# Attention on one core: paired projections, key copies and means on ScalarE, sums set per block

## The chip, the cores and the metric

The kernel runs on one core of a Trainium2 chip. The metric is the device time of one execution in microseconds (us), less is better. Four engines matter here: TensorE (PE) multiplies matrices from SBUF into PSUM, VectorE (DVE) does elementwise arithmetic, ScalarE (ACT) does functions such as exp and copies, and SyncE (SP) issues transfers. Each engine runs its own queue of instructions in order and waits on semaphores for the others.

## The reference

The input x has the shape (16, 384, 16, 16) in fp32. Four layers follow each other.

```
L0  attention over 2 groups of 8 frames: N = 2048 tokens, 12 heads of 32
    qk = xt @ qk_w.T;  v = xt                      (values are the input itself)
    attn = softmax(q k^T / sqrt(32))
    attn = alpha * I + beta * attn - gamma / N     (per head)
    out  = attn @ v
L1  y = depthwise 7x7(x);  layer norm over channels
    y = gelu(y @ w1 + b1)                          (384 -> 1536)
    y = grn(y)       norms of each channel over the pixels, relative to their mean
    x = x + y @ w2 + b2                            (1536 -> 384)
L2  Sobel x and y, 1x1 fusion (768 -> 384), layer norm, gelu, x = x + ...
L3  bn, 1x1, depthwise 3x3, bn, 1x1, residual; linear attention with
    phi(t) = exp(0.5 (2t - t^2)), 8 heads of 48, residual; layer norm, MLP, residual
```

## The kernel before

The input is held as 8 blocks (b, i) of 512 columns, 4 for each of the 2 groups, each as three tiles of 128 channels. Everything is fp32. A matmul of fp32 shows as two instructions in the profile. All engine work is issued through the helper `InOrder` (line 97), which pins each engine's program order to the order of emission, so almost all rows of the profile carry L97 and are told apart by their tiles.

**Attention** (`attention`, lines 395 to 586). There are 6 units (2 groups by 3 sets of 128 channels, 4 heads each). A unit has 4 blocks of 512 queries (numbered 0 to 23 over all units), and a block has 16 key steps. In a key step `scores` makes the scores of 4 heads (tiles st, two banks each, from a pool of 3), and ScalarE turns the two tiles into exponentials e. Then `weighted` works on the step before: 4 matmuls into av, and two VectorE adds that sum the exponentials of several steps into s. `ADDS` (line 56) says how many steps are summed into one group: 4 everywhere before. A group's sum goes through matmuls with ones into dn, the softmax denominators: four quarters of 128 columns in four later steps, or the whole 512 columns in step 2 of the next block for a block's last group (lines 496 to 506). A dictionary `due` holds what is to be emitted at a later step. At the end of a block ScalarE copies av (va) and scales x (xg), step 2 of the next block copies dn (r), and VectorE inverts and scales in the steps behind it; ScalarE passes over r once more (junk) with an accumulated sum as a check of the range.

Queries and keys of the next unit are projected meanwhile: `SLOTS` (line 32) names the key steps of each of a unit's blocks behind which one projection stands (3 fp32 matmuls into the first bank of a tile of the same pool of 3, then a copy: queries on ScalarE, keys on VectorE). The values are transferred as they are. `channel_means` (lines 225 to 238) sums the channels for the gamma term on VectorE, for both groups.

The function `fill` (lines 1466 to 1496) slips other work into the attention's steps where a model of VectorE's time (`pace`) leaves room: first the 7x7 convolution of the blocks (0, 0) and (0, 1) in single VectorE and ScalarE instructions, and, once block (0, 0) is done, its normalization (task l1_0_0; sums su and sv on TensorE).

**The rest** is a list of tasks for every block: l1 (layer 1), mid (layers 2 and 3 up to the linear attention), l3c (the last MLP), and the remaining convolutions. `Plan.all` (line 181) orders them before the kernel is built: of the operations that can start within `SLACK` of the earliest, it takes that of the task with the smallest `RANK`. The MLP weights are loaded in turns: `TURNS` (line 35) lists which layer's weights are in and for which blocks, and `AFTER` delays the convolution's later tiles until a named operation is done. Names used below: ph and po are the first and second MLP matmul, gs is the sum over gelu outputs and pg its matmul, pc and pd are the 1x1 convolutions of layer 3, s0_l, su_l and sv_l belong to a layer norm.

A second branch of the program, a general attention for inputs out of range, is not executed.

Of the kernel before, what the change touches and what calls it, by code (L numbers as in the profile page):

```python
# [15 lines left out]
P = 128  # L16
# [12 lines left out]
NBLK = N // BLK  # L29
NIP = NBLK  # L30
NQC = N // P
SLOTS = ((0, 4, 8), (0, 4), (0, 4), (0,))
FIRST = NQC + 10

TURNS = (
    (0, ((0, 0), (0, 1), (0, 2),)),
    (1, ((0, 0),)),
    (0, ((0, 3),)),
    (1, ((0, 2),)),
    (0, ((1, 0),)),  # L40
    (1, ((0, 1),)),
    (0, ((1, 1), (1, 2), (1, 3),)),
    (1, ((0, 3), (1, 0), (1, 3), (1, 2), (1, 1),)),
)
AFTER = ('hid', 0, 2, 1)

RANK = {
    "mid": ((-2.0, 20.2, -65.9, 40.3), (11.6, 63.7, 50.6, 36.1)),
    "l1": ((-41.0, 15.6, 6.7, 64.2), (55.1, 56.5, 16.9, 27.6)),
    "l3c": ((32.8, 24.4, 106.0, 83.3), (3.4, 80.2, 74.5, 60.5)),  # L50
    "conv": 100.5,
}
SLACK = 0.151
JUNK = 2

ADDS = (4,) * 24
XB, YB, SB = 12, 2, 22
TB = BLK // P
RB = 2 * HW
# [27 lines left out]
class InOrder:  # L87


    def __init__(self, tc, engine):  # L90
        self.tc, self.engine, self.last = tc, engine, None
# [103 lines left out]
def pace(t):  # L195


    n, i = divmod(t - 1, NQC)
    adds = ADDS[n]
    stride = adds // 4  # L200
    pe, dve = 2.066, 2.275 if t and i % adds else 0.0
    at = i - adds - 1
    if at >= 0 and at % adds % stride == 0 and at % adds < 4 * stride and i > adds:
        pe += 0.22
    elif i == 1 and n > 0:
        pe += 0.87
    else:
        pe += 0.09
    if n > 0:
        dve += {2: 0.88, 3: 0.88, 4: 0.88, 5: 0.88, 6: 0.6, 7: 0.66}.get(i, 0.0)  # L210
    return pe, dve


class Task:


    def __init__(self, name, rank, ops):
        self.name, self.rank, self.ops, self.at = name, rank, ops, None
        self.head = next(ops, None)

    def advance(self):
        self.at, self.head = self.head, next(self.ops, None)


def channel_means(dve, pool, X, cols, b):


    parts = pool.tile([P, NC, NBLK], F32, tag="parts", name=f"parts_{b}")
    gm = pool.tile([P, NC], F32, tag="gm", name=f"gm_{b}")

    def part(n):
        dve.tensor_reduce(parts[:, :, n], X[b][n], AX.X, ALU.add)

    def whole():
        dve.tensor_reduce(gm, parts, AX.X, ALU.add)
        dve.scalar_tensor_tensor(gm, gm, -1.0 / N, cols("gamma"), ALU.mult, ALU.mult)

    return gm, [*(lambda n=n: part(n) for n in range(NBLK)), whole]


# [147 lines left out]
def attention(tc, X, xt, L0, block, small, col, cols, ones, load_qk, banks, fill, bound):  # L388
# [6 lines left out]
    with ExitStack() as actx:  # L395
# [15 lines left out]
        def projections(b, g):  # L411


            made = {w: [None] * NBLK for w in "qkv"}
            u = b * NC + g

            def qk(j, n):
                w = "qk"[j]
                pp = bank2(f"p{w}_{u}_{n}")
                for c in range(NC):  # L420
                    pe.matmul(
                        pp[:, 0, :],
                        wqk_sb[:, g, j, c, :],
                        X[b][n][:, c, :],
                        start=(c == 0),
                        stop=(c == NC - 1),
                    )
                o = made[w][n] = small(f"{w}_{u}_{n}")
                (act.copy if j == 0 else dve.tensor_copy)(o, pp[:, 0, :])
                return 2.7 - 0.6 * j  # L430

            def values(n):
                o = made["v"][n] = small(f"v_{u}_{n}")
                nc.sync.dma_start(o, xt[b, g, n])

            def key(n):
                values(n)
                return qk(1, n)

            step = lambda f, *a: lambda: f(*a)  # L440
            early = [step(key, 0), step(qk, 0, 0)] + [step(key, n) for n in range(1, NBLK)]
            late = [step(qk, 0, n) for n in range(1, NBLK)]
            return made, early, late

# [109 lines left out]

            return scores, weighted

        means = [channel_means(dve, op, X, cols, b) for b in range(NB)]
        for b, (_, steps) in enumerate(means):
            for i, s in enumerate(steps):
                due[b * NC * NBLK * NQC - 36 * b + 3 * i] = [s]  # L560
        made, early, late_steps = projections(*units[0])
        for s in early:
            s()
        before = None
        for u, (b, g) in enumerate(units):
            steps = late_steps
            scores, weighted = unit(u, made, means[b][0][:, g : g + 1])
            if u + 1 < len(units):
                made, early, late_steps = projections(*units[u + 1])
                steps = steps + early  # L570
            for n in range(NBLK):
                for t in range(NQC):
                    es = scores(n, t)
                    added = 0.0
                    if before:
                        before()
                    before = lambda f=weighted, a=(n, t, es): f(*a)
                    if t in SLOTS[n]:
                        added = steps.pop(0)() if steps else 0.0
                    fill((u * NBLK + n) * NQC + t, added)  # L580
            assert not steps
        before()
# [7 lines left out]
def conv_seq_kernel(  # L590
# [862 lines left out]
    for b in range(NB):  # L1453
        for i in range(NBLK):
            tasks.append(Task(f"mid_{b}_{i}", rank("mid", b, i), chain(layer2(b, i), layer3a(b, i), layer3b(b, i))))
            tasks.append(Task(f"l3c_{b}_{i}", rank("l3c", b, i), layer3c(b, i)))
            tasks.append(Task(f"l1_{b}_{i}", rank("l1", b, i), layer1(b, i)))
    lead = next(t for t in tasks if t.name == "l1_0_0")

    if fast:  # L1460
        open_pool("s", SB)
# [4 lines left out]
        def fill(t, added=0.0):  # L1466


            nonlocal lag
            if t < 0:  # L1470
                while plan.step(bias):
                    pass
                return
            if t % NQC == 9 and t > NQC:
                u, i = divmod(t // NQC - 1, NBLK)
                plan.mark(("l0", u // NC, i, u % NC))
            length, work = pace(t)
            free = length + added - work - lag
            if NC * NBLK * NQC - 36 < t <= NC * NBLK * NQC - 21 and t % 3 == 1:
                free -= 1.7  # L1480
            if ("y", 0, 0, NC - 1) in plan.made and t % 4 == 1 and plan.holds(lead, "wa"):
                if plan.step(lead) and lead.at.engine == "DVE":
                    free -= lead.at.length
            ops = []
            while t >= FIRST and ("y", 0, YB - 1, NC - 1) not in plan.made:
                op = conv.head
                if op.engine == "DVE":
                    if free < 0.4:
                        break
                    free -= op.length + 0.12 * (op.after[0] in ops[-1:])  # L1490
                if not plan.step(conv):
                    break
                ops.append(op)
                if op.engine == "ACT" and conv.head.engine == "DVE":
                    break
            lag = max(0.0, -free)

        attention(
# [133 lines left out]
```

## Time and profile before

| | |
|---|---|
| median of 3 runs | 2678.43 us (2677.66 to 2680.42) |
| profiled execution | 2678.47 us |
| its span | 2676.6 us |
| granted TensorE clock, mean | 0.997 |
| TensorE busy | 2644.7 us (99%) |
| VectorE busy | 1994.4 us (75%) |
| ScalarE busy | 1559.3 us (58%) |
| attention (first score matmul to last denominator) | 21.96 to 1044.70 us |

Busy times are shares of the span; matmuls are pipelined, so a busy TensorE is not a TensorE at its peak. A row of a group reads: line, engine, operation, output tile <- input tiles with their shapes, count | busy time, mean of one in ns | idle time of the engine just before, and what ended it. A row of the timeline reads: start, length in us, engine and operation, count, and in brackets an idle time before it with its releaser.

### The profile page before, as it was taken

To read this page: it belongs to the slowest core of one execution; us is meant where nothing else is said; L and a number is where in the kernel's file an instruction comes from. 1 tells how busy PE (TensorE), PEld (TensorE's weight loads), DVE (VectorE), ACT (ScalarE), POOL (GpSimd) and SP (SyncE) were. 2 spreads that over 40 slices of the span, in tenths; PEclk is the share of its full clock that TensorE was granted. 3 is DMA by queue.
4 is the path that set the end of the run, shared out by engine and by line. 5 is a ranking of instruction groups with operands and counts; after the bars stand their busy time and mean duration, and the time that the engine had idled before them with its cause. 6 is when DMAs were issued, how large, how long until landed. Compare 5 with 4: busy or idle time off the path is not lost. (4 is left out here: it accounts for less than half of the span.)

```text
span 2676.6 us, 33769 instructions
## 1 busy us (share of the span) xinstructions
PE 2644.7 (99%) x13477; PEld 1066.7 (40%) x13477; DVE 1994.4 (75%) x2586; ACT 1559.3 (58%) x2281; POOL 7.4 (0%) x54
## 2 busy tenths in 40 slices
PE   9999999999999999999999999999999999999999
PEld 3333333333333333345444444445454444454443
DVE  5899999999999999899999659999805545213120
ACT  5787787877888787555635472533664733025221
POOL 0000000000000000000000000000000000000000
PEclk9999999999999999999999999999999999999999
DMA  3000000000000003000101111121000110000000
GB/s 150 1 17 1 5 13 1 17 1 5 13 1 1 13 1 130 0 0 12 36 24 36 48 47 59 59 71 47 24 0 0 36 36 0 12 1 12 12 6 19
DMA packets 34422, 65.19 MB, mean 24 GB/s; under 512 B 1872, under 2 KB 17360, under 8 KB 34256
## 3 DMA queue, kind: packets, MB, share of 16 engines
q1 hardware_dynamic: 34112, 62.79, 7.1%
q8 instruction: 108, 1.77, 0.3%
q14 instruction: 58, 0.48, 0.1%
q10 hardware_dynamic: 144, 0.15, 0.0%
HBM read 56.64 MB, written 6.29 MB: 24 GB/s over the span
## 5 line engine op out<-in xcount | busy, mean ns | idle before, releaser
L97 ACT ACTIVATE e<-st 128x1024 f32<-128x1024 f32 x768 | 744.4, 1022 | 164.3 <-PE st L97 159.3
L97 DVE SCALAR_TENSOR_TENSOR y<-l,vec,y 128x420 f32<-128x420 f32 (+8 forms) x1152 | 658.8, 633 | 7.0 <-ACT y L97 2.3
L97 PE MATMUL st<-q,k 32*128 32x512 f32 x3072 | 457.8, 640 | 1.5 <-DVE k L97 0.6
L97 DVE TENSOR_TENSOR s<-s,e 128x1024 f32<-128x1024 f32 x384 | 445.0, 1211 | 2.9 <-ACT e L97 2.9
L97 PE MATMUL av<-e,v 128*32 128x512 f32 x3072 | 410.0, 605 | 0.5 <-ACT va L97 0.5
L97 PE MATMUL ph_l<-y,wa 128*128 128x512 f32 x576 | 260.9, 599 | 0.1
L97 PE MATMUL ph_l3c<-d_l3c,wa 128*128 128x512 f32 x576 | 257.5, 593 | 0.0
L97 PE MATMUL po_l<-hid_l,wb 128*128 128x512 f32 x576 | 253.2, 593 | 2.5 <-ACT hid_l L97 2.5
L97 PE MATMUL po_l3c<-hid_l3c,wb 128*128 128x512 f32 x576 | 253.9, 593 | 0.0
L97 DVE TENSOR_TENSOR s<-e,e 128x1024 f32<-128x1024 f32 x192 | 225.8, 1217 | 27.3 <-PE dn L97 14.3
L97 ACT ACTIVATE hid_l3c<-ph_l3c,vec 128x512 f32<-128x512 f32 x96 | 65.7, 685 | 252.2 <-PE ph_l3c L97 251.9
L97 PEld LDWEIGHTS st<-q,k 32*128 32x128 f32 x3072 | 135.7, 183 | 159.7 <-issue 100.5
L97 PEld LDWEIGHTS av<-e,v 128*32 128x32 f32 x3072 | 60.5, 108 | 292.0 <-issue 283.7
L97 PEld LDWEIGHTS po_l<-hid_l,wb 128*128 128x128 f32 x576 | 109.2, 190 | 139.2 <-issue 130.6
L97 PEld LDWEIGHTS ph_l<-y,wa 128*128 128x128 f32 x576 | 109.2, 191 | 136.5 <-issue 128.7
L97 PEld LDWEIGHTS ph_l3c<-d_l3c,wa 128*128 128x128 f32 x576 | 108.9, 190 | 136.7 <-issue 130.5
L97 PEld LDWEIGHTS po_l3c<-hid_l3c,wb 128*128 128x128 f32 x576 | 108.7, 190 | 133.5 <-issue 130.1
L97 PEld LDWEIGHTS dn<-s,ones 128*32 128x32 f32 x2496 | 81.9, 110 | 186.1 <-issue 170.9
L97 PE MATMUL dn<-s,ones 128*32 128x128 f32 (+1 forms) x2496 | 141.9, 297 | 0.2 <-DVE s L97 0.2
L97 ACT ACT_TABLE_LOAD x102 | 130.9, 1283 | 10.3 <-PE ph_l L97 7.4
L97 DVE SCALAR_TENSOR_TENSOR o_l3c<-po_l3c,vec,l 128x512 f32<-128x512 f32 x24 | 17.7, 746 | 158.3 <-PE po_l3c L97 157.6
L97 ACT ACTIVATE hid_l<-ph_l,vec 128x512 f32<-128x512 f32 x96 | 65.6, 684 | 116.0 <-PE ph_l L97 115.5
(155 smaller groups left out, 2479.7 us busy)
## 6 DMA issues: line engine op xcount, KB each, us to landing
wa<-in_w_dram SPq DMA_DIRECT2D x12, 768.0 KB, 4.5
wb<-in_w_dram SPq DMA_DIRECT2D x12, 768.0 KB, 4.7
wa<-in_mlp_w_dram SPq DMA_DIRECT2D x12, 768.0 KB, 4.4
wb<-in_mlp_w_dram SPq DMA_DIRECT2D x12, 768.0 KB, 4.5
x<-in_x_dram SPq DMA_DIRECT2D x8, 768.0 KB, 10.8
v<-in_xt_dram SPq DMA_DIRECT2D x24, 256.0 KB, 2.7
out_dram<-o_l3c SPq DMA_DIRECT2D x24, 256.0 KB, 2.0
qkv<-in_qkv_wT_dram SPq DMA_DIRECT2D x3, 576.0 KB, 11.0
```

Of the source, the lines that this page charges most:

```text
L97: self.last = self.tc.keep_in_program_order(make(*args, **kw))
```

## The change

The same quantities are computed; what is emitted, where, and on which engine differs. Projections are emitted in pairs into the two banks of one tile, behind key step 5 of a block, and both copies come after both sets of matmuls, both on ScalarE (`project`). The second group's channel means become twelve ScalarE passes with accumulation, one every two steps from step 156 on. `ADDS` takes a value for each of the 24 blocks. `fill` handles the normalizations of both convolved blocks (`leads`) from step `LEAD` on, and counts the parts of a denominator (`pace`). `TURNS`, `AFTER`, `RANK` and `SLACK` of the work behind the attention have other values.

```diff
@@ -29,31 +29,30 @@
 NBLK = N // BLK
 NIP = NBLK
 NQC = N // P
-SLOTS = ((0, 4, 8), (0, 4), (0, 4), (0,))
+SLOT = 5
+LEAD = 20 * NQC + 6
 FIRST = NQC + 10
 
 TURNS = (
-    (0, ((0, 0), (0, 1), (0, 2),)),
-    (1, ((0, 0),)),
-    (0, ((0, 3),)),
+    (0, ((0, 0), (0, 1), (0, 2), (0, 3),)),
+    (1, ((0, 0), (0, 1),)),
+    (0, ((1, 0), (1, 2),)),
     (1, ((0, 2),)),
-    (0, ((1, 0),)),
-    (1, ((0, 1),)),
-    (0, ((1, 1), (1, 2), (1, 3),)),
-    (1, ((0, 3), (1, 0), (1, 3), (1, 2), (1, 1),)),
+    (0, ((1, 1), (1, 3),)),
+    (1, ((1, 0), (0, 3), (1, 2), (1, 1), (1, 3),)),
 )
-AFTER = ('hid', 0, 2, 1)
+AFTER = ('x4', 0, 2)
 
 RANK = {
-    "mid": ((-2.0, 20.2, -65.9, 40.3), (11.6, 63.7, 50.6, 36.1)),
-    "l1": ((-41.0, 15.6, 6.7, 64.2), (55.1, 56.5, 16.9, 27.6)),
-    "l3c": ((32.8, 24.4, 106.0, 83.3), (3.4, 80.2, 74.5, 60.5)),
-    "conv": 100.5,
+    "mid": ((36.6, 22.0, 24.3, 85.6), (18.6, 42.9, 96.6, 26.9)),
+    "l1": ((50.1, 89.5, 75.2, 4.0), (51.1, 16.8, 81.7, 28.5)),
+    "l3c": ((45.7, 99.2, 100.9, 121.0), (-20.9, -6.3, 70.9, 62.0)),
+    "conv": 109.4,
 }
-SLACK = 0.151
+SLACK = 0.196
 JUNK = 2
 
-ADDS = (4,) * 24
+ADDS = (16, 8, 16, 16, 4, 4, 4, 2, 2, 8, 16, 16, 4, 16, 2, 4, 16, 8, 4, 4, 4, 4, 4, 4)
 XB, YB, SB = 12, 2, 22
 TB = BLK // P
 RB = 2 * HW
@@ -197,11 +196,11 @@
 
     n, i = divmod(t - 1, NQC)
     adds = ADDS[n]
-    stride = adds // 4
     pe, dve = 2.066, 2.275 if t and i % adds else 0.0
     at = i - adds - 1
-    if at >= 0 and at % adds % stride == 0 and at % adds < 4 * stride and i > adds:
-        pe += 0.22
+    parts = sum(j * adds // 4 == at % adds for j in range(4)) if at >= 0 else 0
+    if parts:
+        pe += 0.22 * parts
     elif i == 1 and n > 0:
         pe += 0.87
     else:
@@ -214,15 +213,16 @@
 class Task:
 
 
+
     def __init__(self, name, rank, ops):
-        self.name, self.rank, self.ops, self.at = name, rank, ops, None
+        self.name, self.rank, self.ops, self.rest = name, rank, ops, 0
         self.head = next(ops, None)
 
     def advance(self):
-        self.at, self.head = self.head, next(self.ops, None)
-
-
-def channel_means(dve, pool, X, cols, b):
+        self.head = next(self.ops, None)
+
+
+def channel_means(dve, pool, X, cols, b, act=None):
 
 
     parts = pool.tile([P, NC, NBLK], F32, tag="parts", name=f"parts_{b}")
@@ -230,11 +230,21 @@
 
     def part(n):
         dve.tensor_reduce(parts[:, :, n], X[b][n], AX.X, ALU.add)
+
+    def chunk(n, c):
+        junk = pool.tile([P, BLK], F32, tag="junk", name=f"mean_{b}_{n}_{c}", bufs=1)
+        act.activation(
+            junk, X[b][n][:, c, :], AF.Identity, accum_out=parts[:, c, n : n + 1]
+        )
 
     def whole():
         dve.tensor_reduce(gm, parts, AX.X, ALU.add)
         dve.scalar_tensor_tensor(gm, gm, -1.0 / N, cols("gamma"), ALU.mult, ALU.mult)
 
+    if act:
+        return gm, [
+            *(lambda n=n, c=c: chunk(n, c) for n in range(NBLK) for c in range(NC)), whole
+        ]
     return gm, [*(lambda n=n: part(n) for n in range(NBLK)), whole]
 
 
@@ -414,30 +424,28 @@
             made = {w: [None] * NBLK for w in "qkv"}
             u = b * NC + g
 
-            def qk(j, n):
+            def qk(j, n, pp):
                 w = "qk"[j]
-                pp = bank2(f"p{w}_{u}_{n}")
                 for c in range(NC):
                     pe.matmul(
-                        pp[:, 0, :],
+                        pp,
                         wqk_sb[:, g, j, c, :],
                         X[b][n][:, c, :],
                         start=(c == 0),
                         stop=(c == NC - 1),
                     )
                 o = made[w][n] = small(f"{w}_{u}_{n}")
-                (act.copy if j == 0 else dve.tensor_copy)(o, pp[:, 0, :])
-                return 2.7 - 0.6 * j
+                return lambda: act.copy(o, pp)
 
             def values(n):
                 o = made["v"][n] = small(f"v_{u}_{n}")
                 nc.sync.dma_start(o, xt[b, g, n])
 
-            def key(n):
+            def key(n, pp):
                 values(n)
-                return qk(1, n)
-
-            step = lambda f, *a: lambda: f(*a)
+                return qk(1, n, pp)
+
+            step = lambda f, *a: lambda pp: f(*a, pp)
             early = [step(key, 0), step(qk, 0, 0)] + [step(key, n) for n in range(1, NBLK)]
             late = [step(qk, 0, n) for n in range(1, NBLK)]
             return made, early, late
@@ -554,13 +562,19 @@
 
             return scores, weighted
 
-        means = [channel_means(dve, op, X, cols, b) for b in range(NB)]
+        means = [channel_means(dve, op, X, cols, b, act if b else None) for b in range(NB)]
         for b, (_, steps) in enumerate(means):
             for i, s in enumerate(steps):
-                due[b * NC * NBLK * NQC - 36 * b + 3 * i] = [s]
+                due[b * NC * NBLK * NQC - 36 * b + (3 - b) * i] = [s]
+        def project(name, steps):
+            pp = bank2(name)
+            for copy in [f(pp[:, i, :]) for i, f in enumerate(steps)]:
+                copy()
+            return 2.7 * len(steps)
+
         made, early, late_steps = projections(*units[0])
-        for s in early:
-            s()
+        for i in range(0, len(early), 2):
+            project(f"p_{i}", early[i : i + 2])
         before = None
         for u, (b, g) in enumerate(units):
             steps = late_steps
@@ -575,8 +589,9 @@
                     if before:
                         before()
                     before = lambda f=weighted, a=(n, t, es): f(*a)
-                    if t in SLOTS[n]:
-                        added = steps.pop(0)() if steps else 0.0
+                    if t == SLOT and steps:
+                        added = project(f"p_{u}_{n}", steps[:2])
+                        del steps[:2]
                     fill((u * NBLK + n) * NQC + t, added)
             assert not steps
         before()
@@ -1455,7 +1470,7 @@
             tasks.append(Task(f"mid_{b}_{i}", rank("mid", b, i), chain(layer2(b, i), layer3a(b, i), layer3b(b, i))))
             tasks.append(Task(f"l3c_{b}_{i}", rank("l3c", b, i), layer3c(b, i)))
             tasks.append(Task(f"l1_{b}_{i}", rank("l1", b, i), layer1(b, i)))
-    lead = next(t for t in tasks if t.name == "l1_0_0")
+    leads = [next(t for t in tasks if t.name == f"l1_0_{i}") for i in range(YB)]
 
     if fast:
         open_pool("s", SB)
@@ -1476,23 +1491,28 @@
                 plan.mark(("l0", u // NC, i, u % NC))
             length, work = pace(t)
             free = length + added - work - lag
-            if NC * NBLK * NQC - 36 < t <= NC * NBLK * NQC - 21 and t % 3 == 1:
-                free -= 1.7
-            if ("y", 0, 0, NC - 1) in plan.made and t % 4 == 1 and plan.holds(lead, "wa"):
-                if plan.step(lead) and lead.at.engine == "DVE":
-                    free -= lead.at.length
-            ops = []
-            while t >= FIRST and ("y", 0, YB - 1, NC - 1) not in plan.made:
-                op = conv.head
-                if op.engine == "DVE":
-                    if free < 0.4:
+            for task in (*leads, conv):
+                if task.rest > t or t < (FIRST if task is conv else LEAD):
+                    continue
+                before = None
+                while task is not conv or ("y", 0, YB - 1, NC - 1) not in plan.made:
+                    op = task.head
+                    if before and before.engine != op.engine:
+                        task.rest = t + 1 + (before.engine == "DVE")
                         break
-                    free -= op.length + 0.12 * (op.after[0] in ops[-1:])
-                if not plan.step(conv):
-                    break
-                ops.append(op)
-                if op.engine == "ACT" and conv.head.engine == "DVE":
-                    break
+                    if op.engine == "DVE":
+                        if free < max(0.4, op.length - 1.5):
+                            break
+                        free -= op.length + 0.12 * (before in op.after)
+                    if not plan.holds(task, "wa") or not plan.step(task):
+                        break
+                    if op.engine in ("ACT", "PE"):
+                        before = op
+                        if task.head.engine == "ACT" and task is not conv:
+                            task.rest = t + 1
+                            break
+                    elif op.engine:
+                        before = op
             lag = max(0.0, -free)
 
         attention(
```

## The prediction

> **What bounds the kernel now.** First read: the busy shares of the whole span. TensorE is busy 99%, so a microsecond is gained or lost only if its queue gets shorter or longer, or if it stands idle. Second read: the busy time by stretches (columns: stretch; its length; PE, PEld, DVE, ACT, POOL busy with counts; clock; DMA share; GB/s). The first stretch is the attention, 1022.74 us.
>
> ```profile
> PE 2644.7 (99%) x13477; PEld 1066.7 (40%) x13477; DVE 1994.4 (75%) x2586; ACT 1559.3 (58%) x2281; POOL 7.4 (0%) x54
> 21.96:1044.70 1022.74, 1020.53 (x8903) 324.03 (x8902) 954.46 (x1023) 822.27 (x946) 0.00 (x0) 1.00 0.03 8
> 1175.00:1500.00 325.00, 323.38 (x973) 151.96 (x972) 319.19 (x498) 177.81 (x288) 1.99 (x14) 1.00 0.08 25
> ```
>
> In the attention VectorE is 93% busy, and from 1175 to 1500 it is 98% busy: a second bound stands close behind TensorE. Third read: the timeline of TensorE (start, length, work). It shows what a key step costs.
>
> ```profile
> 27.87 1.31 PE L97 MATMUL st<-q,k 32*128 32x512 f32 x8
> 30.11 1.14 PE L97 MATMUL st<-q,k 32*128 32x512 f32 x8
> 32.17 1.31 PE L97 MATMUL st<-q,k 32*128 32x512 f32 x8
> ...
> 577.75 1.14 PE L97 MATMUL st<-q,k 32*128 32x512 f32 x8
> ...
> 580.04 2.84 PE L97 MATMUL pk<-x,wqk_sb 128*128 128x512 f32 x6
> 582.81 1.14 PE L97 MATMUL st<-q,k 32*128 32x512 f32 x8
> ...
> 585.10 1.16 PE L97 MATMUL st<-q,k 32*128 32x512 f32 x8
> ...
> 588.03 1.14 PE L97 MATMUL st<-q,k 32*128 32x512 f32 x8
> ...
> 1003.19 1.14 PE L97 MATMUL st<-q,k 32*128 32x512 f32 x8
> 1005.48 1.14 PE L97 MATMUL st<-q,k 32*128 32x512 f32 x8
> 1006.85 1.06 PE L97 MATMUL av<-e,v 128*32 128x512 f32 x8 [0.23 <-ACT va L97]
> 1008.06 1.52 PE L97 MATMUL st<-q,k 32*128 32x512 f32 x8
> 1011.37 1.14 PE L97 MATMUL st<-q,k 32*128 32x512 f32 x8
> ```
>
> A bare step (scores and weighted values only) takes 2.24 and 2.06 us in turn (27.87, 30.11, 32.17), mean 2.15: there are three two-bank score tiles, so every other time the second tile waits for an exponential. A step with one quarter of a denominator takes 2.29 (1003.19 to 1005.48): the quarter alone is 0.22 longer than nothing, but it hides that wait, so taking it away saves 2.29 − 2.15 = 0.13, not 0.22. The other two groups are the same block boundary with a projection at key step 0 (block 13) and without one (block 23). With it, steps 1 and 2 take 2.29 and 2.93 (582.81, 585.10, 588.03; step 2 holds a whole denominator, 0.87); without it 2.58 and 3.31 (1005.48, 1008.06, 1011.37). On ScalarE the copies va and xg stand there between the exponentials. So a projection at step 0 costs 2.77 by itself (6 × 0.43 + 0.21 changeover) but gives back 0.29 + 0.38 = 0.67: 2.10 net.
>
> **The change, part by part.** All is summed against the profiled execution, 2678.47 us (span 2676.6, 1.9 outside it), 0.04 above the median of the runs.
>
> *Pairs at step 5.* 43 projections lie among the steps. Before: 21 at step 0 at 2.10 and 22 at steps 4 and 8 at 2.77, 105.0 us. After: 21 pairs and one single. A pair is 12 × 0.43 = 5.16; its changeover (0.21) and the score-tile wait that the pause lets the exponentials catch up on (0.17 in a bare step) nearly cancel. 21 × 5.16 + 2.77 = 111.1. So +6.1: 21 changeovers fewer, but 20 boundaries lose their cover.
>
> *Keys copied on ScalarE.* 24 copies leave VectorE and join ScalarE.
>
> ```profile
> L97 DVE COPY k<-pk 128x512 f32<-128x512 f32 x24 | 16.3, 678 | 44.9 <-PE pk L97 44.9
> L97 ACT COPY q<-pq 128x512 f32<-128x512 f32 x24 | 14.0, 585 | 47.5 <-PE pq L97 47.5
> L97 DVE TENSOR_REDUCE parts<-x 128x3 f32<-128x1536 f32 x8 | 14.0, 1745 | 0.0
> L97 ACT ACTIVATE junk<-r 128x512 f32<-128x512 f32 x24 | 15.2, 633 | 3.5 <-DVE r L97 3.5
> ```
>
> TensorE saves nothing: the 44.9 us are VectorE's waits, and no row shows TensorE waiting for a projection's tile. The two copies (2 × 0.49 when back to back) sit in a step in which ScalarE would be idle for 3 us; the next scores (1.1 us) hide them. Without that cover, 21 × 0.49 = +10. The Trainium skill, "ScalarE: Activation LUTs", "Rules for kernel authors", tells one to keep simple arithmetic on VectorE rather than ScalarE, which speaks against this edit; its reason is a bf16 mode. Here the fp32 copy is shorter on ScalarE (585 against 678 ns), so the row decides, and the rule would make no difference to the sum.
>
> *Means of the second group on ScalarE.* Four VectorE reduces (7.0 us) become 12 ScalarE passes with an accumulated sum; nearest row junk, about 0.72 with its read-out. They stand in blocks 9 to 11, whose steps are mostly bare after the change. Each delays an exponential there by between 0 (fully hidden) and 0.72. In before, a ScalarE piece of the convolution in a bare step makes it 2.48 instead of 2.24; that row gives 12 × 0.24 = +2.9, range 0 to +8.6.
>
> *Adds per block.* Denominators are summed over groups of 16, 8, 4 or 2 steps: 81 groups of four-head matmuls instead of 96. Relative to groups of 4: groups of 16 remove 12 quarters, 12 × 0.13 = 1.6 less, but the ScalarE check pass (junk) now falls into a bare step (+0.3): −1.3 a block; groups of 8 remove 8 quarters: −1.0; groups of 2 have 16 more quarters, two in a step, at about 0.18: +2.9 each. Seven blocks of 16, three of 8, three of 2: −9.1 − 3.0 + 8.7 = −3.4. VectorE pays for it: 30 more adds (36.3) less copies (16.3) and reduces (7.0), +13.0, for which 14 convolution steps (8.9) leave the attention. By block, rows summed, VectorE then needs 40.2 to 43.5 in the blocks of 16, where TensorE needs 41.6. In two or three of the seven it is late; I take +1.
>
> *Normalizations.* The order of instructions shows l1_0_0's in blocks 20 to 23, as before, and l1_0_1's sums still behind the last step: in this the change does not do what its name says. Its steps lengthen blocks 20 to 22 now by 3.4, 1.9 and 3.3 us (48.83 where a first block of a unit takes 45.40; 39.67 and 41.04 where the step lengths above sum to 37.8); I take no change (±3).
>
> Attention: +6.1 + 2.9 − 3.4 + 1 = +6.6.
>
> *Behind the attention.* The convolution has 33 VectorE steps left there (19 before), 8.9 us more. The transition before:
>
> ```profile
> 1071.62 1.10 PE L97 MATMUL su_l<-s_l,ones 128*128 128x512 f32 x2 [1.44 <-DVE s_l L97]
> 1078.56 1.12 PE L97 MATMUL sv_l<-s_l,ones 128*128 128x512 f32 x2 [0.69 <-DVE s_l L97]
> 1086.98 0.56 PE L97 MATMUL pg_l<-gs_l,ones 128*128 128x2 f32 x2 [4.72 <-DVE gs_l L97]
> 1087.65 5.39 PE L97 MATMUL ph_l<-y,wa 128*128 128x512 f32 x6
> ```
>
> TensorE idles 6.9 us, and after the 4.72 six matmuls take 5.2 instead of 2.6 (half the clock): 9.4 lost. After: all 12 first MLP tiles stand ahead of su_l1_0_1, and the input of pg no longer waits behind l1_0_1's reciprocal (VectorE's sums reach su, pg and sv 0.7 before to 1.2 after TensorE's). The order takes away the long idle, the added convolution brings some back. The second MLP matmul starts 48.2 us after the last denominator now; I expect 46. The Trainium skill, "TensorE: Matmul & The Clock Gate", Part 1, lets the clock halve after one idle window of some 3.4 us; by it an idle below that would keep the clock, and the 2.6 would be saved whole. Next, VectorE's and ScalarE's work between sv_l2_0_0 and pc_l3a_0_0 has 11.2 us of TensorE work beside it where it has 8.8 now: −2. Over the whole tail TensorE's own work sums to 1599 us (0.43 for each 512-column instruction), and it takes 1626 (and 6 for the last output): it falls 27 behind. Of this the later part should lose 2: VectorE idles less early, but its work stays within 2 us of TensorE's until 310 us and within 4 to 16 of it until 800, where before it was 50 ahead from 515 on. Tail: −2 − 2 − 2 = −6, range −12 to +8. Weight loads fall from 48 to 36, and table loads by 15 (1.28 each): both stand beside TensorE work (DMA share 0.03 to 0.19, ScalarE 58%) and count zero; a late 768 KB group would cost its 4.5 us landing each time.
>
> 2678.5 + 6.6 − 6 = **2679**.
>
> **Rivals.** *A plain count holds (faster).* 15 groups fewer × 4 quarters × 0.22 = −13.1 and 21 changeovers × 0.21 = −4.4, with the boundaries' and the means' ScalarE work hidden: attention −17.5, tail −3: 2658. For it: ScalarE is only 80% busy in the attention. Against it: the bare steps at 27.87 to 32.17 and the uncovered boundary at 1005, which already show the waits that this count leaves out.
>
> *VectorE becomes the bound (slower).* It decides where VectorE's work plus its own idle exceeds TensorE's. Before, VectorE idled 14.7 us in the first 47 us behind the attention and 22.4 by 241. If it idles so again, TensorE at 302 us is 1.3 + 22.4 + 1.7 = 25 late, where it was 19: +6 instead of −6. In the blocks of 16, 1.5 us of idle each would make seven blocks 2 us late: +14 less the 1 taken. 2679 + 12 + 4 (a third of that 13, since the lighter blocks between catch up) = 2695. For it: 93% and 98% above. Against it: the blocks of 2 and 4 between those of 16 have 2 to 6 us spare.
>
> **How the numbers follow.** The main case 0.48 (2671 to 2688), the plain count 0.22 (2650 to 2667), VectorE 0.30 (2686 to 2704). A measurement of this kernel tells about 0.2% (5.4 us) from no change. Main: 0.2 of it below 2673, 0.26 above 2684. Faster 0.22 + 0.10 = 0.32; slower 0.28 + 0.12 = 0.40; same 0.28. The range 2660 to 2697 leaves out about 2 in 10.
>
> **What would show it.** Right: blocks of 16 near 41.6 us, of 4 near 42.9, of 2 near 45.8; steps 1 and 2 of nearly every block 0.3 and 0.4 longer than under a projection; attention 1027 to 1031; no idle above 3 us at pg. Wrong: a pair's step below 7.0, boundaries at 2.3 (plain count); s rows of TensorE's dn waiting for DVE, or pc and pd waits growing behind 1100 us (VectorE); the blocks with means above 44.

## The result and the profile after

The changed kernel takes 2674.85 us (median of 20 runs, 2674.17 to 2679.83), the kernel before 2679.14 (20 runs, 2677.64 to 2680.64): the ratio is 0.999 with the interval 0.9983 to 0.9997. So it is faster by about a tenth of a per cent, a small difference but one clear of the noise; the forecast was no change (2679).

The 20 times are not spread over that range. Twelve lie between 2674.17 and 2675.64 with a mean clock of 0.997, eight between 2678.89 and 2679.83 with 0.995 or 0.996. The profile taken with them shows one of the eight (2679.38); the run `e1_again` below is the same kernel and has a time of the lower group (2674.66). Both are needed:

| us | before | changed, upper group | changed, lower group |
|---|---|---|---|
| first score matmul | 21.96 | 22.07 | 21.84 |
| attention, to the first MLP matmul | 1022.77 | 1030.27 | 1027.01 |
| tail, to the end of the last matmul | 1625.67 | 1619.06 | 1617.88 |
| last output | 6.20 | 6.19 | 6.15 |
| span | 2676.60 | 2677.59 | 2672.88 |

The attention got longer and the tail shorter. The busy line of the page and the stretches that the prediction read, here of the changed kernel's upper profile, with the attention of the lower profile as the last line:

```profile
PE 2644.6 (99%) x12997; PEld 1061.5 (40%) x12997; DVE 2011.5 (75%) x2588; ACT 1557.5 (58%) x2314; POOL 7.4 (0%) x54
22.07:1052.34 1030.27, 1021.94 (x8423) 318.45 (x8423) 962.66 (x1013) 837.38 (x992) 0.00 (x0) 1.00 0.03 8
1182.00:1507.00 325.00, 322.00 (x947) 148.15 (x946) 317.75 (x513) 173.17 (x329) 1.58 (x11) 0.99 0.05 15
21.84:1048.85 1027.01, 1018.73 (x8424) 317.78 (x8423) 962.03 (x1013) 836.57 (x992) 0.00 (x0) 1.00 0.03 8
```

The attention has 480 TensorE instructions fewer (13477 to 12997 in the whole kernel), yet TensorE's busy time in it fell only from 1020.53 to 1018.73 us in the lower profile: most of the time of the removed denominators is now waiting inside other rows. The timeline of TensorE in block 6 (groups of 4, upper profile) shows where:

```profile
276.21 1.14 PE L96 MATMUL st<-q,k 32*128 32x512 f32 x8
277.58 1.07 PE L96 MATMUL av<-e,v 128*32 128x512 f32 x8 [0.23 <-ACT va L96]
278.80 1.52 PE L96 MATMUL st<-q,k 32*128 32x512 f32 x8
282.11 1.14 PE L96 MATMUL st<-q,k 32*128 32x512 f32 x8
284.17 1.31 PE L96 MATMUL st<-q,k 32*128 32x512 f32 x8
286.41 1.14 PE L96 MATMUL st<-q,k 32*128 32x512 f32 x8
288.48 5.42 PE L96 MATMUL p<-x,wqk_sb 128*128 128x512 f32 x12
293.83 1.14 PE L96 MATMUL st<-q,k 32*128 32x512 f32 x8
```

(Rows between these are left out.) Steps 1 and 2 of the block take 2.59 and 3.31, the uncovered boundary; then 2.06, 2.24, and the step with the pair 7.42, which is 2.24 and 5.18. From the first scores of a block to those of the next, in the lower profile, blocks of 4 take 42.87 to 42.93 (up to block 19, before the normalization), blocks of 16 between 41.62 and 43.16, and blocks of 2 between 45.80 and 46.05; block 0, with no boundary ahead of it, takes 40.61.

Now the place that makes most of the gap between the two groups: block 22, where the square root of l1_0_0's normalization stands on ScalarE behind va and xg, with a table load of 1.28 us on either side. The rows are the scores of step 2, in two halves, and what follows them. First the upper profile, then the lower.

```profile
972.17 1.13 PE L96 MATMUL st<-q,k 32*128 32x512 f32 x4 [0.83 <-ACT s_l L96]
974.50 2.08 PE L96 MATMUL st<-q,k 32*128 32x512 f32 x4 [1.21 <-ACT e L96]
976.51 1.94 PE L96 MATMUL av<-e,v 128*32 128x512 f32 x8
978.22 1.93 PE L96 MATMUL dn<-s,ones 128*32 128x512 f32 x8
```

```profile
971.79 1.13 PE L96 MATMUL st<-q,k 32*128 32x512 f32 x4 [0.83 <-ACT s_l L96]
974.13 1.13 PE L96 MATMUL st<-q,k 32*128 32x512 f32 x4 [1.21 <-ACT e L96]
975.19 1.06 PE L96 MATMUL av<-e,v 128*32 128x512 f32 x8
976.07 1.04 PE L96 MATMUL dn<-s,ones 128*32 128x512 f32 x8
```

The waits are the same to the hundredth (0.83 and 1.21). Behind them the same matmuls take twice as long in the one execution. The clock column of the stretches says why: 0.76 in the first, 1.00 in the second.

```profile
968.10:982.60 14.50, 12.46 (x70) 3.12 (x66) 8.78 (x6) 10.76 (x13) 0.00 (x0) 0.76 0.00 1
```

```profile
967.70:979.10 11.40, 9.36 (x68) 2.50 (x64) 7.33 (x5) 10.65 (x13) 0.00 (x0) 1.00 0.00 1
```

Block 22 takes 44.27 and 41.16. Of the 4.7 us between the two groups these are 3.1; 1.2 lie in the tail, where only the upper profile has a further stretch at half clock (1288.2 to 1291.6), and 0.4 elsewhere.

Why the clock falls in one and not in the other can be read from the traces. In every kept profile the stretches at half clock begin whole multiples of 3.413 us apart, and all but the last, which the end of the kernel cuts off, last 3.41 us or a multiple of it. (In the upper profile they begin at 974.16, 1090.2 and 1288.2, which are 34 and 58 such windows apart.) So the clock changes only at the ends of windows of 3.41 us, which stand still within one execution. These are the windows about the two waits, first of the upper profile, then of the lower, where they are counted back from the stretch that begins at 1086.0:

```profile
970.75:974.16 3.41, 1.71 (x16) 0.43 (x8) 2.01 (x1) 3.37 (x4) 0.00 (x0) 1.00 0.00 0
974.16:977.58 3.42, 3.08 (x12) 0.90 (x16) 3.42 (x3) 3.08 (x4) 0.00 (x0) 0.50 0.02 5
977.58:980.99 3.41, 3.41 (x19) 0.71 (x12) 2.45 (x4) 0.76 (x3) 0.00 (x0) 0.50 0.00 0
```

```profile
969.95:973.36 3.41, 2.14 (x20) 0.56 (x12) 1.59 (x1) 3.37 (x4) 0.00 (x0) 1.00 0.00 0
973.36:976.78 3.42, 2.65 (x20) 0.72 (x20) 3.42 (x3) 3.42 (x4) 0.00 (x0) 1.00 0.02 5
```

In the upper profile one window holds nearly all of both waits, TensorE is busy for 1.71 of its 3.41 us, and the clock is halved in the next two. In the lower profile the second wait is divided between two windows, busy for 2.14 and 2.65, and the clock stays. The Trainium skill, "TensorE: Matmul & The Clock Gate", Part 1, says that the chip watches activity in a window of some 3.4 us that runs freely, so that the same kernel can meet it at another phase in each run. The traces agree with this. The prediction's reading that an idle of less than 3.4 us would keep the clock does not hold here, since windows of which TensorE was busy for half were followed by half clock.

Twelve other kept profiles have the same two waits at this place. Together with these two, four have no half clock behind them (block 22 takes 41.15 or 41.16), seven have 3.41 us of it (42.79 to 42.84) and three have 6.83 (44.12 to 44.45). In front of the half clock the window at this place is busy for 41 to 65%; where none follows, the emptiest window is busy for 63 to 65%. Over all kept profiles no half clock begins behind a window that is busy for more than 66%, and behind those of 60% or less it begins in 65 of 85. So a window with many idle moments is needed, but the busy share alone does not decide. The place has three outcomes, and the gap of 4.7 is read from the two profiles shown; for the other 19 executions of the changed kernel only the time and the mean clock are known, and they fit.

Behind the attention, upper profile:

```profile
1089.16 1.10 PE L96 MATMUL su_l<-s_l,ones 128*128 128x512 f32 x2 [3.65 <-DVE s_l L96]
1092.19 0.59 PE L96 MATMUL pg_l<-gs_l,ones 128*128 128x2 f32 x2 [1.93 <-DVE gs_l L96]
1094.90 2.05 PE L96 MATMUL sv_l<-s_l,ones 128*128 128x512 f32 x2 [2.13 <-DVE gmean_l L96]
1096.97 3.70 PE L96 MATMUL po_l<-hid_l,wb 128*128 128x512 f32 x4
```

The idle is not gone but has moved from pg (4.72) to su (3.65), with pg and sv behind it: together 7.7 where it was 6.9. In both groups sv and the first po run at half clock. The second MLP matmul starts 44.6 us (45.2 in the lower group) behind the attention, 48.2 before.

### The profile page after: what moved, and what is told of

It is laid out like the page before. It is cut to its first block, busy times and chain, and to the rows that moved or that the text cites. A ratio compares the mean times of both kernels' runs of the same rounds, so it can differ in the third digit from the quotient of the medians.

```text
span 2677.6 us, 32803 instructions
## 1 busy us (share of the span) xinstructions
PE 2644.6 (99%) x12997; PEld 1061.5 (40%) x12997; DVE 2011.5 (75%) x2588; ACT 1557.5 (58%) x2314; POOL 7.4 (0%) x54
## 5 line engine op out<-in xcount | busy, mean ns | idle before, releaser
L96 DVE TENSOR_TENSOR s<-s,e 128x1024 f32<-128x1024 f32 x444 | 513.3, 1216 | 11.7 <-ACT e L96 11.2
L96 PE MATMUL st<-q,k 32*128 32x512 f32 x3072 | 474.1, 641 | 4.0 <-ACT e L96 2.3
L96 PEld LDWEIGHTS st<-q,k 32*128 32x128 f32 x3072 | 146.1, 183 | 220.1 <-issue 132.4
L96 DVE TENSOR_TENSOR s<-e,e 128x1024 f32<-128x1024 f32 x162 | 191.0, 1221 | 54.7 <-ACT e L96 36.0
L96 PE MATMUL p<-x,wqk_sb 128*128 128x512 f32 x288 | 132.3, 610 | 1.2 <-DMA x<-in_x_dram 1.2
L96 DVE SCALAR_TENSOR_TENSOR g_l3a<-h_l3a,dw,g_l3a 128x450 f32<-128x450 f32 (+1 forms) x192 | 119.0, 702 | 4.2 <-ACT g_l3a L96 4.1
L96 PEld LDWEIGHTS dn<-s,ones 128*32 128x32 f32 x2016 | 64.1, 110 | 125.4 <-issue 107.0
```

The costliest lines, as they stand in the source:

```text
L96: self.last = self.tc.keep_in_program_order(make(*args, **kw))
```

## Experiments

Attention and tail are read from each profile as in the table above. "Left" is the number of VectorE steps of the convolution of the first two blocks that run behind the attention, counted in the trace; the expectations of e10 to e16 give numbers higher by 1 or 2.

| run | time, median | attention | tail | left |
|---|---|---|---|---|
| before | 2678.3 to 2679.1 | 1022.8 | 1625.7 | 19 |
| changed (lower / upper group) | 2674.85 | 1027.0 / 1030.3 | 1617.9 / 1619.1 | 33 |
| e2 root later | 2678.59 | 1027.7 | 1621.2 | 34 |
| e3 pair at 0 | 2703.43 | 1019.2 | 1654.2 | 43 |
| e4 singles | 2701.27 | 1019.1 | 1653.1 | 43 |
| e5 pair at 0, same fill | 2689.15 | 1040.8 | 1617.9 | 33 |
| e6 singles, same fill | 2674.32 | 1025.1 | 1617.9 | 33 |
| e7 groups of 4, same fill | 2699.44 | 1049.1 | 1617.8 | 33 |
| e8 keys on VectorE | 2709.28 | 1061.2 | 1619.1 | 33 |
| e9 old order behind | 2728.27 | 1029.9 | 1668.7 | 33 |
| e10 pair at 0, fitted | 2666.63 | 1016.4 | 1621.3 | 34 |
| e11 singles, fitted | 2682.68 | 1020.2 | 1634.6 | 29 |
| e12 groups of 4, own fill | 2805.2 | 1038.4 | 1738.1 | 0 |
| e13 means on VectorE | 2678.74 | 1028.7 | 1620.6 | 33 |
| e14 pair at 0, step 0.03 longer | 2664.39 | 1016.9 | 1617.9 | 33 |
| e15 as e14, means on VectorE | 2667.86 | 1020.3 | 1617.9 | 33 |
| e16 pair at 0, groups of 4 | 2680.72 | 1020.1 | 1631.3 | 20 |

**e1_again.** No edit.

> The changed kernel once more, for a second profile. Its 20 runs fall into two groups, 12 near 2674.6 (mean clock 0.997) and 8 near 2679.3 (0.995 to 0.996); the profile taken shows one of the upper group. Theory A (half clock): a profile of the lower group (span near 2673) has the same instructions at the same steps, and lacks the half-clock stretch behind the root of the normalization l1_0_0 in block 22 (step 1 about 5 us instead of 7.9), or the one at sv and the first po behind the attention. Rival B (a wait that falls one way or the other on ScalarE or VectorE): the clock is 1.0 in both stretches of both profiles and the 4.7 us lie in a wait elsewhere, for example at the first loads or in the last 300 us. If the profile is of the upper group again (span near 2677.5), it should agree with the first within 0.5 us in every stretch.

Theory A held for block 22: the profile is the lower one shown above, the same instructions without the half clock there. The half clock at sv and the first po is in both.

**e2_root_later.**

```diff
                     op = task.head
+                    if op.table and t % NQC in (14, 15, 0, 1, 2, 3):
+                        break
```

> The changed kernel, but the square root of a normalization in the attention (with its two table loads on ScalarE) is not emitted at steps 14 to 3 of a block; it moves from step 0 of block 22, right behind va and xg, to step 4. Theory A: the 8 us of lateness in steps 0 and 1 of block 22 become about 3.3 as before the change, no half clock follows, and the time is near 2670 in one group. If the half clock is only behind the attention, the two groups remain, both 3 us lower (2671.5 and 2676). Rival B: no change beyond 2 us, since the normalization costs the same wherever it stands, and two groups remain.

Ratio 0.9996 (0.9987 to 1.0005). Block 22 takes 41.80, without the half clock, but the table loads still hold the exponentials up: the block is 4.0 us over its step lengths (37.75), where the lower profile of the changed kernel is 3.4 over them. The tail became 1621.2, with 13.65 us at half clock at its start (10.24 in the changed kernel) and 3.41 more at 1288. The gap of 4 us between two groups is gone, but the times lie at 2677 to 2679: half of theory A, and no gain.

**e3_pair_at_0 and e4_singles.**

```diff
-SLOT = 5
+SLOT = 0
```

```diff
-SLOT = 5
+SLOTS = ((0, 4, 8), (0, 4), (0, 4), (0,))
...
-                    if t == SLOT and steps:
-                        added = project(f"p_{u}_{n}", steps[:2])
-                        del steps[:2]
+                    if t in SLOTS[n] and steps:
+                        added = project(f"p_{u}_{n}_{t}", steps[:1])
+                        del steps[:1]
```

> The changed kernel with the pairs behind key step 0 instead of step 5. My step: 20 block boundaries regain their cover (0.67 each), so the attention gets 13 us shorter (1017 instead of 1030), less what moves: the normalization l1_0_0 comes later and 10 more convolution steps (6.3 us of VectorE) are left behind the attention. Time 2662 to 2668. Plain count: the place of the pair makes no difference, 2674 to 2679.

> The changed kernel with single projections at the key steps where they stood before (0, 4, 8), all copies on ScalarE. My step: attention 8 us shorter than with pairs at step 5 (1022), 10 more convolution steps behind it, time 2667 to 2673. Plain count: 21 changeovers more, +4.4 us, 2679 to 2684.

The attention got 8 us shorter in both, as expected of the second; of the first, 13 were expected. The whole got 22 to 25 us longer than the kernel before (ratios 1.0088 and 1.0081). The planner put less convolution into the shorter attention and found another order behind it, and in that order TensorE waits: 1654 instead of 1618. These two runs tell nothing of the pair's place by their times.

**e5 to e7: the same order of all else.** The planner is told the same added time at step 5 as in the changed kernel; only the instructions in question move. For e5 and e7 (e6 emits its singles as e4 does):

```diff
-                    if t == SLOT and steps:
-                        added = project(f"p_{u}_{n}", steps[:2])
+                    if t == 0:
+                        later = project(f"p_{u}_{n}", steps[:2]) if steps else 0.0
                         del steps[:2]
+                    if t == SLOT:
+                        added = later
```

```diff
+FOURS = (4,) * 24
...
-            adds = ADDS[u * NBLK : (u + 1) * NBLK]
+            adds = FOURS[u * NBLK : (u + 1) * NBLK]
```

> The changed kernel with the pairs behind key step 0, but the time that they add is told to the planner at step 5 as before, so that the convolution, the normalization and everything behind the attention keep their order (33 convolution steps left, as in the changed kernel). My step: the boundaries regain their cover, attention 13 us shorter (1014 to 1017), the tail within 3 us of the changed kernel's, time 2660 to 2667. Rival (VectorE is the bound behind the planned order): VectorE has 962 us of work in the attention and falls late in the blocks of 16; what TensorE gains at the boundaries comes back as waits of dn for s or behind the attention, time 2671 to 2679.

> The changed kernel with single projections at the old key steps (0, 4, 8), all copies on ScalarE, planner told as with pairs at step 5. My step: attention 8 us shorter (1019 to 1022), tail the same, time 2665 to 2671. Plain count (21 changeovers more): 2679 to 2684. VectorE as the bound: 2673 to 2679.

> The changed kernel with sums over groups of 4 in all blocks, planner told as with the changed groups, so that all other order stays. My step: the attention gets 2.8 us longer on TensorE (1030 in the faster group), VectorE has 36 us less to do in it; time 2677 to 2680. Plain count: 15 groups more, +13 us, 2687 to 2692. VectorE as the bound: its 36 us come free in the attention, time no longer than the changed kernel's or shorter, 2668 to 2675.

The tails are 1617.8 to 1617.9, so the attention alone moved: +13.8, −1.9 and +22.1 against the lower group. None of the three came out as its step lengths said. In e5 blocks 5, 6, 18 and 19 take 44.6 to 45.0 instead of the 42.4 that they take in e14, and block 9 takes 47.8 instead of 42.6: the convolution steps that were dealt to a 7 us step 5 now stand in a 2 us step, the adds behind them come late, and a denominator waits. Its row, and that of e14 where the same steps are dealt anew:

```profile
L96 PE MATMUL dn<-s,ones 128*32 128x128 f32 x1824 | 90.2, 274 | 10.6 <-DVE s L96 10.4
```

```profile
L96 PE MATMUL dn<-s,ones 128*32 128x128 f32 x1824 | 85.1, 273 | 0.0
```

In e6 the same thing costs less: blocks 7, 15 and 19 take 1.4 to 2.3 us longer than in e4, where the same singles are dealt by their own places, and 2 of the expected 5 to 8 us are left.

In e7 VectorE has 34 us less to do (928.6 busy in the attention, 962.0 in the changed kernel), and yet blocks 7 and 8 take 49.1 and 50.2 instead of 46.1 and 45.9. With groups of 2 the planner had dealt them some 20 us of convolution each beside 19.5 us of adds; with groups of 4 the adds are 26.8 and 29.1 us, and VectorE is idle for 1.9 and 0.8 us only. Blocks 9 to 11 and 13 to 15 are longer than 42.87 as well (43.4 to 45.1). Where nothing is late, e7 gives the price of a block directly: blocks 2, 3 and 16, which have groups of 16 in the changed kernel, take 42.87 instead of 41.62 (+1.25), and blocks 1 and 17, with groups of 8 there, take 0.9 longer.

**e8_keys_on_vector.**

```diff
-                return lambda: act.copy(o, pp)
+                return lambda: (act.copy if j == 0 else dve.tensor_copy)(o, pp)
```

> The changed kernel with the key copies back on VectorE; the order of everything else is the same. My step: TensorE doesn't wait for these copies, within 1.5 us of the changed kernel (2673 to 2676 and the upper group 4.7 higher). Rival: VectorE stands before a pair's end (up to 5 us, 45 us of such waits in the kernel before) while sums and the convolution queue behind it; with its 93% in the attention that costs 5 to 15 us, 2680 to 2690.

+34 us, all but 1.2 of it in the attention; beyond the rival's 15. VectorE's timeline of one pair, with TensorE's pair at 248.68:

```profile
247.59 1.76 DVE L96 RECIPROCAL r<-r 128x128 f32<-128x128 f32 x2
254.75 0.69 DVE L96 COPY k<-p 128x512 f32<-128x512 f32 x1 [5.40 <-ACT q L96]
255.36 4.95 DVE L96 SCALAR_TENSOR_TENSOR y<-l,vec,y 128x480 f32<-128x480 f32 x7
260.22 2.36 DVE L96 TENSOR_TENSOR s<-e,e 128x1024 f32<-128x1024 f32 x2
```

VectorE stands for 5.4 us in front of a copy of 0.69, and the seven convolution steps meant for that time come after it, ahead of the adds. Summed over the 24 copies VectorE waits 68.9 us, 57.1 of them in the attention. The work was not dealt anew for this run, so the 34 us are the price of these waits with the changed kernel's dealing, not of the engine as such: in the kernel before, 44.9 us of such waits made no block late.

**e9_old_order_behind.** The changed kernel with `TURNS`, `AFTER`, `RANK` and `SLACK` of the kernel before.

> The changed kernel with TURNS, AFTER, RANK and SLACK of the kernel before. The attention is the same instruction for instruction (1027 or 1030 us); only the order behind it differs. If the new constants are what makes the tail 6.6 to 7.8 us shorter, the tail is back at 1625 and the time at 2679 to 2684. If the tail is shorter because of what the attention hands over (all 12 first MLP tiles ahead, another amount of convolution), it stays within 2 us of 1618 and the time of 2675. By the sums of VectorE's work against TensorE's in the order (at most 4 us late between 310 and 600 us behind the attention, 1.7 in the changed kernel) I expect 1619 to 1622.

Wrong by 46 us. Constants that give 1625.7 behind the old attention give 1668.7 behind the new one, though VectorE's work summed in the order is hardly late anywhere. TensorE idles for 44.1 us in this tail, 12.9 in the changed kernel's lower profile; the longest sums are in front of sv (8.0), po (7.6, for hid), zb (7.3) and pg (5.4). It runs for 51.2 us at half clock before the last output, where the lower profile has 10.24, which costs 20 us. So the 51 us are 31 of waits and 20 of the half clock.

**e10, e11, e12: planned with their own place.** e10 is e3 with `pe, dve = 2.076` in `pace` (2.066 before), e11 is e4 with 2.086, e12 has `ADDS = (4,) * 24`.

> The changed kernel with pairs behind key step 0, planned with that place, and with the planner's length of a key step 0.01 us longer, by which 36 convolution steps are left behind the attention and not 45. The order behind the attention then has VectorE 2.4 us late at most. If the fit of VectorE's work to the steps decides, the attention is 1017 to 1021 and the tail 1618 to 1622: time 2664 to 2669. If VectorE is the bound as such (its 962 us plus waits), 2672 to 2680.

> The changed kernel with single projections at the old key steps, planned with those places, the planner's key step 0.02 us longer (31 convolution steps left). Attention 1018 to 1022; VectorE 5.6 us late at most behind it, tail 1619 to 1626; time 2664 to 2672. If VectorE is the bound as such: 2673 to 2680.

> The changed kernel with groups of 4 in all blocks, planned as such: one convolution step is left behind the attention, and the sum for the second normalization (su of l1_0_1) stands in its last block. My step: attention 3 us longer than the changed kernel's by TensorE's steps and up to 3 more for the second normalization (1030 to 1034); the tail loses the idle at its start (8 us) and more slack on VectorE, 1606 to 1616; time 2662 to 2674. Plain count: 13 us more for 15 more groups, 2685 and up.

e10: ratio 0.9954 (0.994 to 0.9967); a planner's constant changed by 0.01 turns 2703 into 2667. e11: the attention as expected, the tail 9 us above its range. e12: far off on both counts (ratio 1.0471). With no convolution step left VectorE has little to do at the start of the tail (18.2 busy of 50 us), the order is another one, and the tail is 120 us longer. TensorE's waits in it sum to some 100 us (44 in e9) and its stretches at half clock to 116; which of them follow from which is not shown.

**e13 to e16.** e13 is the changed kernel with `channel_means(dve, op, X, cols, b)` for both groups, one reduce every three steps; e14 is e3 with `pe, dve = 2.096`; e15 is both; e16 is e3 with `ADDS = (4,) * 24`.

> The changed kernel with the second group's means back on VectorE (four reduces of 1.75 us); all other order is the same. My term: the 12 ScalarE passes cost 2.9; by the blocks as measured (9 to 11 at 41.98, 42.94 and 42.19 where the step lengths give 41.9, 41.7 and 41.7) it is 1.8. So 2672 to 2673 in the lower group (2677 in the upper). Rival: VectorE has no room for 7 us there, since the planner no longer counts them, and its lateness costs 2 to 8 us: 2676 to 2683.

> Pairs behind key step 0 as in the run before, but with the planner's key step 0.03 us longer: 35 convolution steps are left, and the order behind the attention is that of the changed kernel. If the fit still holds: attention 1016 to 1018, tail 1617.9 to 1619.1 as in every kernel with this order: 2661 to 2665. If VectorE gets late (as with the planner told of step 5): over 2670.

> The same with the means back on VectorE. My term: 1.8 to 2.9 us shorter than with the means on ScalarE. Rival: VectorE late in blocks 9 to 11, 2 to 8 us longer.

> Pairs behind key step 0 and groups of 4 in all blocks, planned as such (planner's key step as in the changed kernel): 22 convolution steps left, VectorE up to 7.9 us late between 120 and 310 us behind the attention. The attention by the step lengths is 3.7 us longer than with the set groups (1020 to 1022); the tail, with an order near the changed kernel's, 1620 to 1630: 2666 to 2677. If the set groups were worth the plain count, the attention would be 13 us longer (1030).

e14 beats both kernels: 2664.39, ratio 0.9946 (0.9933 to 0.996). The means on VectorE cost 1.7 us of attention in e13 and 3.4 in e15 (block 10 takes 45.81 there instead of 42.23): both rivals held, my term had the wrong sign. `fill` no longer counts the reduces in these two runs, so what they would cost with a place of their own is not shown. The tail of e13 is 2.7 longer as well, with 17 us at half clock instead of 10. In e16 the attention is 3.2 us longer than in e14, as the step lengths say (3.7), not 13; the tail, with another order, lost the rest.

## Why the prediction was wrong, step by step

**The step that failed** is the sentence on the normalization, "I take no change (±3)", and with it the idea that one profiled execution stands for all. The step lengths of blocks 20 to 22 sum to 120.9 before and 121.2 after; the blocks took 129.54 before, and take 127.12 in the lower group and 130.24 in the upper. So the normalization cost 8.6 before and costs 5.9 or 9.0. By block it was 3.4, 1.9 and 3.3 before and is 1.2, 1.3 and 3.4 in the lower group: where its work stands now, blocks 20 and 21 lose less (no run isolates which of the moved instructions does it). In block 22 the upper group has 3.1 more for the half clock. The prediction weighed the half clock only behind the attention, where it stayed; it decides in block 22, where the root now stands next to va and xg. Block 23, for which the prediction has no price, is 0.7 longer, with three ScalarE passes of the same normalization (0.82 to 0.85 each) now in its first three steps.

The second term that was too small is the tail, sized at −6: it came to −6.6 and −7.8. In the lower profile the normalization (−2.7, less the 0.7 of block 23) and the tail (1.8 below its −6) make up most of the 4.4 us by which it lies below the forecast sum. That the sum holds to half a microsecond in the upper group (eight runs near 2679.3) is partly luck: there the half clock, which the sum doesn't have at this place, takes back what the normalization saved. The median lies in the lower group, with twelve of the twenty runs, 4.3 below the kernel before.

**Pairs at step 5**, +6.1: right in size. Dealt anew, singles at the old steps give an attention 6.8 (e11) or 7.9 (e4) shorter than the lower group's, and pairs at step 0 (e14) 10.1 shorter, or 11.8 without the 1.7 us of half clock that e14 has in block 22. The boundary's cover is what counts, not the changeovers. By block it is worth less than the 0.67 taken: blocks of 4 take 42.43 with the pair at step 0 and 42.87 with it at step 5.

**Groups**, −3.4: right (e16 against e14: 3.2, and a block of 16 saves 1.25 in e7 where 1.3 was taken). The plain count of 13 is ruled out.

**Keys**, 0: right against the kernel before, where no block was late, but the reasoning missed what hangs on it. "The 44.9 us are VectorE's waits" was read as costing nothing; with pairs, and the work dealt as in the changed kernel, such waits come with 34 us more of attention (e8).

**Means**, +2.9: mis-sized and one-sided. Blocks 9 to 11 show +1.8 above their step lengths (counted from key step 1 to key step 1, since step 0 of block 9 still holds quarters of block 8), and the same work on VectorE, not counted by `fill`, costs 1.7 to 3.4 more.

**VectorE late**, +1: about 2, as what is left over. Blocks 1 to 19 take 817.0 in the lower profile where the step lengths give 813.3; 1.8 of the 3.7 are the means.

**Behind the attention**, −6: the amount nearly right, its shape in part. The idle of 4.72 at pg went, as said, but 3.65 at su took its place. The waits for pc's input, which the prediction wanted 2 shorter, went from 4.4 to 1.2. Over the whole tail, with the same number of TensorE instructions, TensorE idles for 12.9 us in the lower profile and 16.9 before, and is busy for 1605.0 and 1608.7. That the sums of VectorE's work in the order bound the tail was too simple: e9 is at most 4 us late by these sums and lost 51. Why the new constants and the new attention go together is not settled here; the runs show that the old constants behind the new attention are worse (e9), and the new constants behind the old attention were not run.

**The rivals.** The plain count (its 60 quarters at 0.22 are 13.2, not 13.1) is refuted by the blocks of e7 and by e16. VectorE as the bound did not happen in the changed kernel, where no denominator's matmul waits for s, but it is what the misfits e5, e7 and e8 show: it is decided not by the sum of its work (e7 had less) but by whether each step's share fits the step.

## What to carry to other kernels

Where a second engine is busy 93% beside the first and work is dealt to it step by step, a part's worth can't be read from the time of a run in which the dealing no longer fits. Hold the order of all else, then deal anew, and in both read the blocks in which nothing is late. Read a step's price as the difference of two step lengths in the trace, not as the instructions' own time: removing 240 matmuls in the attention was worth 3 us, moving the pairs back to the block boundaries 10. When times fall into two groups, take a profile of each before explaining a difference as small as the gap between them.

## What was not expected of the hardware

The clock of TensorE halved after two waits of 0.83 and 1.21 us, neither of them long, and in other executions with the same instructions and the same waits it did not. The traces tie it to how the waits fall into windows of 3.41 us: one busy for 1.71 us was followed by half clock, and two busy for 2.14 and 2.65 were not. It costs 3.1 us in block 22, and in some runs 1.7. A wait in front of a copy of 0.69 us on VectorE, in an otherwise full queue, came with a longer loss (34 us over 24 copies) than all the matmuls that the change removed were worth.
